# Routing tokens to experts beside a recurrence: one indirect DMA at a time, expert weights by register-addressed loads, uneven blocks

## The chip, the cores and the metric

The kernel runs on one core of a Trainium2 chip. Such a core has five engines that run their own instruction streams: TensorE (PE; its weight loads are shown as PEld), VectorE (DVE), ScalarE (ACT), GpSimd (POOL) and SyncE (SP). Semaphores order them. DMAs are issued from an engine's queue; here SP and ACT issue plain ones, POOL the indirect ones, whose row addresses come from a tile in SBUF. The metric is the device time of one execution in microseconds (us), lower is better. The granted TensorE clock is shown by the profile as a share of full speed (PEclk).

## The reference, cut to what matters

The whole program is two transformer-like layers. The change touches only its last stage, a recurrence (8 batches by 512 steps, width 256) followed by a mixture of 16 experts, of which each token uses two.

```python
def _L1_cond2_ref(x, h0, Wx, Wh, b):
    xW = jnp.einsum('ntd,dh->nth', x, Wx) + b
    def step(h_prev, xw_t):
        h_next = jnp.tanh(xw_t + h_prev @ Wh)
        return (h_next, h_next)
    _, hs = jax.lax.scan(step, h0, jnp.swapaxes(xW, 0, 1))
    return jnp.swapaxes(hs, 0, 1)

def _L1_ffn_ref(x, gate_w, gate_b, shared_wg, shared_wu, shared_wd, experts_wg, experts_wu, experts_wd):
    router_logits = jax.nn.sigmoid(x @ gate_w + gate_b)
    expert_values, expert_indices = jax.lax.top_k(router_logits, k=2)
    expert_values = expert_values / jnp.sum(expert_values, axis=-1, keepdims=True)
    hg = jnp.einsum('bsd,edi->bsei', x, experts_wg)
    hu = jnp.einsum('bsd,edi->bsei', x, experts_wu)
    all_outputs = jnp.einsum('bsei,eid->bsed', jax.nn.silu(hg) * hu, experts_wd)
    selected = jnp.take_along_axis(all_outputs, expert_indices[..., None], axis=2)
    expert_weighted = jnp.sum(expert_values[..., None] * selected, axis=2)
    return x + _mlp(x, shared_wg, shared_wu, shared_wd) + expert_weighted
```

The recurrence is strictly serial in time. The experts need only its outputs, so they can run on an earlier stretch of time while later steps are computed. Each of 8 x 512 = 4096 tokens goes to two experts: 8192 rows of 256 numbers.

## The kernel before

All earlier stages end shortly before 3779 us of the profile's span and stay as they are, except that line numbers shift. The last stage is `rnn_moe`.

**A step.** `rnn_step` issues for each time step 8 small products on PE (L1272, 16 matmul records in fp32), a tanh on ACT (L1276) and a 32-wise transposition on DVE (L1277) that writes the new state into a ring; the next step's products wait for that transposition. `rnn_seed` (L1256) loads the next step's input term into PSUM ahead of time. So one step is a loop PE, ACT, DVE, PE.

**Pieces between steps.** Everything else is written as Python generators that are advanced once after each step. A generator that yields 1 has put a piece of PE work behind this step; one that yields 0 has not. After each step one piece of `ranks`, one of `gathers`, and one of `chunks` or, when that gives no PE work, of `big` is taken. The order on PE, ACT and DVE is exactly the order in which this is written; SP and POOL take their instructions in program order too. What a piece wants done on ACT or DVE is put off with `later` to the time just after the next step.

- `rnn_project`: the input product of each later chunk of 16 steps (2 pieces each).
- `Experts.chunk`: for 16 finished steps (128 tokens): POOL copies the state into `hT` (L1308) and the input into `xc` (L1235); PE computes the router logits, turns the state to rows (`hr`, L1326) and computes the shared expert: 4 pieces, the result in `acc`.
- `Experts.rank`: for a block of `TB` = 128 steps (8 chunks, 1024 tokens): DVE counts tokens for each expert and computes `row`, the place of each token in a list sorted by expert in tiles of 128 rows, `wrow`, the row of a tile's weights, and `tw`, the mixing weights. In its middle it issues 16 scatters in one go (L1421, POOL, 128 rows of 1 KB each into the DRAM tensor `xs`).
- `Experts.tiles`: (2 x 1024 + 16 x 127) / 128 = 31 tiles a block. A tile is fetched three tiles ahead: its weights `w` (128 x 768 numbers, 384 KB) by an indirect DMA on POOL (L1456), its rows `x` (128 KB) by SP (L1460). Three pieces a tile: `gate` for k = 0 and k = 1 (L1475, 128 x 256 products), each with half the turning of the next tile's `x` (L1466), and a third with `down` of the tile two before (L1494) and `back`, which turns the activation of the tile before (L1488). SP stores the result (L1499, `ys`).
- `Experts.collect`: the two rows of each token are gathered from `ys` (L1533, POOL, two at a time), added to `acc` with the mixing weights (L1541, DVE), and stored (L1545, SP).

When the 512 steps are over, a loop without steps takes the pieces that are left. At the start of the stage ACT fills both `xs` tensors with zeros (L1562).

Of the kernel before, what the change touches and what calls it, by code (L numbers as in the profile page):

```python
# [18 lines left out]
P = 128  # L19
# [6 lines left out]
TB = 128  # L26
# [1201 lines left out]
NB = S // TB  # L1228
# [10 lines left out]
def rnn_project(K, M):  # L1239

    for n in range(1, S // XB):
        xc = chunk_x(K, M, n, "xp")
        yield 0
        px = M.psx.tile([P, D], F32, name="px", tag="px")
        for k in range(2):
            K.nc.tensor.matmul(px, xc[:, k], M.wx[:, k, :], start=(k == 0), stop=(k == 1))
            if k == 1:
                M.later(lambda n=n, px=px: K.nc.vector.tensor_tensor(M.xw[:, n, :], px, M.rbias, ALU.add))
            yield 1
# [11 lines left out]
def rnn_step(K, M, t):  # L1261
# [15 lines left out]
    nc.vector.transpose(M.ring[:, at].rearrange("p k b -> p (k b)"), h)  # L1277


class Experts:  # L1280
# [11 lines left out]
    def __init__(self, K, M, nb):  # L1292
        self.K, self.M, self.nb = K, M, nb
        self.xs, self.ys = M.xs[nb % 2], M.ys[nb % 2]
        self.hr, self.acc = [], []
        self.top, self.topi = self.rp("top", [8, 8]), self.rp("topi", [8, 8], U32)

    def rp(self, name, shape, dt=F32):
        return self.M.rp.tile([P] + shape, dt, name=name, tag=name)

    def chunk(self, c, ring):
# [3 lines left out]
        t0 = self.nb * TB + c * XB  # L1305
# [11 lines left out]
        for k in range(2):  # L1317
            nc.tensor.transpose(pt[:, k, :], hk[k], K.ident)
        hr = M.ap.tile([P, D], F32, name="hr", tag="hr", bufs=18)
        self.hr.append(hr)  # L1320
        rl = M.sp.tile([P, NE], F32, name="rl", tag="rl")

        def logits():
            nc.vector.tensor_tensor(rl, pr, M.rb, ALU.add)
            nc.scalar.activation(rl, rl, AF.Sigmoid)
            nc.scalar.copy(hr, po[:, 0:D])  # L1326

        later(logits)
        pw = M.pgu.tile([P, 2, P], F32, name="pw", tag="gu")
# [7 lines left out]
        def act():  # L1337
            nc.scalar.activation(a, pw[:, 0], AF.Sigmoid)
            nc.vector.max(out=self.top[:, c, :], in_=rl)
            nc.vector.max_index(out=self.topi[:, c, :], in_max=self.top[:, c, :], in_values=rl)  # L1340
            nc.vector.tensor_tensor(a, pw[:, 0], a, ALU.mult)
# [12 lines left out]
        acc = M.ap.tile([P, D], F32, name="acc", tag="acc", bufs=22)  # L1354
# [11 lines left out]
    def rank(self):  # L1366

        K, M, NE, NT, rp, top = self.K, self.M, self.NE, self.M.NT, self.rp, self.top
        nc, mm, C = K.nc, K.nc.tensor.matmul, TB // XB
# [16 lines left out]
        for d in (1, 2, 4):  # L1386
# [30 lines left out]

        group = f"scatter{self.nb}"
        for c in range(C):
            for i in range(2):  # L1420
                w = nc.gpsimd.indirect_dma_start(  # L1421
                    out=self.xs[:, :],
                    out_offset=bass.IndirectOffsetOnAxis(ap=self.row[:, c, i : i + 1], axis=0),
                    in_=self.hr[c],
                    in_offset=None,
                )
                K.tc.declare_no_dep(w.ins, group=group, reason="rows of their own")
                K.tc.add_to_no_dep_group(group, w.ins)
        yield 0

        le = M.rp.tile([P, NT, NE], F32, name="le", tag="le", bufs=1)
        nc.vector.tensor_tensor(le, end.unsqueeze(1).to_broadcast([P, NT, NE]), M.tile.unsqueeze(2).to_broadcast([P, NT, NE]), ALU.is_le)
# [14 lines left out]

    def tiles(self):

        K, M, NT = self.K, self.M, self.M.NT  # L1450
# [3 lines left out]
        def fetch(m):  # L1454
            W[m] = M.wp.tile([P, 768], F32, name="w", tag="w")
            nc.gpsimd.indirect_dma_start(  # L1456
                out=W[m], out_offset=None, in_=M.experts, in_offset=bass.IndirectOffsetOnAxis(ap=self.wrow[:, m : m + 1], axis=0)
            )
# [13 lines left out]
        def gate(m, k):  # L1472
            if k == 0:
                G[m] = M.pgu.tile([P, 2, P], F32, name="pg", tag="gu")
            mm(G[m].rearrange("p g i -> p (g i)"), X[m][:, k, :], W[m][:, k * D : (k + 1) * D], start=(k == 0), stop=(k == 1))  # L1475
            if k == 1:
                X.pop(m)
                later(lambda: act(m, G.pop(m)))

        def act(m, pg):  # L1480
            a = A[m] = M.sp.tile([P, P], F32, name="ea", tag="ea")
            nc.scalar.activation(a, pg[:, 0, :], AF.Sigmoid)
            nc.vector.tensor_tensor(a, pg[:, 0, :], a, ALU.mult)
            nc.vector.tensor_tensor(a, pg[:, 1, :], a, ALU.mult)

        def back(m):
            pa = M.pd.tile([P, P], F32, name="pa", tag="pd")
            nc.tensor.transpose(pa, A.pop(m), K.ident)  # L1488
            aT = A[m] = M.sp.tile([P, P], F32, name="aT", tag="aT")
            later(lambda: nc.vector.tensor_copy(aT, pa))  # L1490

        def down(m):
            py = M.pd.tile([P, D], F32, name="py", tag="pd")
            mm(py, A.pop(m), W.pop(m)[:, 2 * D : 3 * D], start=True, stop=True)  # L1494
# [10 lines left out]
        yield 1  # L1505
# [3 lines left out]
        for m in range(NT + 2):  # L1509
            for n in range(3):  # L1510
# [5 lines left out]
                if n == 2:  # L1516
                    if 0 <= m - 2 < NT:
                        down(m - 2)
                    if 0 <= m - 1 < NT:
                        back(m - 1)  # L1520
# [4 lines left out]
    def collect(self):  # L1525

        K, M, nc = self.K, self.M, self.K.nc
        C, Y = TB // XB, {}
        for c in range(C + 2):
            if c < C:  # L1530
                for i in range(2):
                    y = Y[c, i] = M.sp.tile([P, D], F32, name="yg", tag="yg", bufs=6)
                    nc.gpsimd.indirect_dma_start(  # L1533
                        out=y, out_offset=None, in_=self.ys[:, :], in_offset=bass.IndirectOffsetOnAxis(ap=self.row[:, c, i : i + 1], axis=0)
                    )
            yield 0
            yield 0
            if c > 1:
                acc = self.acc[c - 2]
                for i in range(2):  # L1540
                    nc.vector.scalar_tensor_tensor(acc, Y.pop((c - 2, i)), self.tw[:, c - 2, i : i + 1], acc, ALU.mult, ALU.add)  # L1541
                    if i == 0:
                        yield 0
                t0 = self.nb * TB + (c - 2) * XB
# [3 lines left out]
def rnn_moe(K, out):  # L1548
# [3 lines left out]
    with ExitStack() as es:  # L1552
        wp = K.pool(es, "m_w")
        M = Scope()
        M.NT = (2 * B * TB + 16 * (P - 1)) // P
# [74 lines left out]
        def ranked(x):  # L1630
            yield from x.rank()
            for _ in range(20):
                yield 0
# [5 lines left out]

        with K.tc.manual_schedule(engines={E.PE, E.Activation, E.DVE}):  # L1640
            for t in range(S):
                at = t % XB
                if t % TB == 0:
                    blk = Experts(K, M, t // TB)
                rnn_step(K, M, t)
                consume()

                advance(ranks)
                advance(gathers)
                advance(chunks) or advance(big)  # L1650
                if at == XB - 1:
                    chunks.append(blk.chunk(t % TB // XB, M.ring))
                    if t % TB == TB - 1:
                        def late(x=blk, ring=M.ring):
                            yield from x.chunk(TB // XB - 1, ring)
                            ranks.append(ranked(x))
                        chunks[-1] = late()
            while chunks or ranks or big or gathers:
# [3 lines left out]
                advance(chunks) or advance(big)  # L1662
            consume()
# [170 lines left out]
```

## Time and profile before

| what | us |
|---|---|
| median of 3 runs (4696.21 to 4704.57) | 4701.56 |
| the profiled execution | 4710.34 |
| its span, first to last instruction | 4708.6 |
| first to last transposition of the step loop, L1277 x512 | 3779.0 to 4548.7 |
| from there to the end of the span | 160 |

The last stage has these operations on POOL, by the groups of that engine from 3779 us on: 124 weight fetches L1456 (mean 963 ns, 119.4 us), 64 scatters L1421 (966 ns, 61.8 us), 64 gathers L1533 (959 ns, 61.4 us), and copies of 0.29 to 0.41 us each. In the timeline each row is start, duration, engine, line, what it writes and reads, and in brackets how long the engine was idle before it and who ended that. In a table of windows each row is a stretch of time, its length, and for each engine busy time and, in brackets, the number of instructions, then the granted clock, the DMA engines' busy share and GB/s. A DMA_INDIRECT row on POOL is the time in which POOL makes the descriptors, not the transfer.

### The profile page before, as it was taken

How to read it: one execution, taken by the hardware profiler on the slowest of the kernel's cores; microseconds unless marked ns; L12 is line 12 of the kernel's file. 1: busy time of each engine (PE TensorE's matmuls, PEld its weight loads, DVE VectorE, ACT ScalarE, POOL GpSimd, SP SyncE). 2: the span in 40 equal slices, each digit the busy share in tenths (PEclk: the TensorE clock that was granted, in tenths of full speed). 3: DMA queues.
4: the chain of work that ended last, by engine and by line, in shares of the span. 5: the costliest groups of instructions: out<-in, count | busy, mean ns of one | idle time of the engine just before them, and what ended most of it. 6: DMA issues, size and time to landing. Idle time of an engine off the chain costs nothing.

```text
span 4708.6 us, 121113 instructions
## 1 busy us (share of the span) xinstructions
PE 3497.0 (74%) x51178; PEld 2153.2 (46%) x51178; DVE 2179.5 (46%) x7763; ACT 1309.7 (28%) x4703; POOL 1019.4 (22%) x1658
## 2 busy tenths in 40 slices
PE   8700067777766767478889999999999976879675
PEld 5400044444444444345545555555555554546453
DVE  3300045555554444444547666667666632334333
ACT  2100012222222222133434334433433321323233
POOL 0177500000000000042102222222222112132434
PEclk9855589999999999989989999999999997989897
DMA  2100000000000000100000000000000021334356
GB/s 77 37 1 1 0 16 17 17 17 12 12 3 3 3 3 3 55 24 20 9 2 1 1 1 1 1 1 1 1 1 1 1 81 48 101 110 135 118 150 223
DMA packets 94415, 153.88 MB, mean 33 GB/s; under 512 B 21264, under 2 KB 72240, under 8 KB 93488
## 3 DMA queue, kind: packets, MB, share of 16 engines
q0 software_dynamic: 28352, 72.05, 5.4%
q1 hardware_dynamic: 54208, 59.69, 4.0%
q10 hardware_dynamic: 11312, 14.42, 0.9%
q8 instruction: 401, 6.57, 0.6%
q14 instruction: 142, 1.16, 0.1%
HBM read 107.82 MB, written 39.45 MB: 31 GB/s over the span
## 4 chain that ended last, share of the span: by engine, by line
PE 53%; DVE 20%; another core or an unknown queue 9%; ACT 8%; issue 7%; DMA 1%; ACTq 0%; POOL 0%; SPq 0%; DVEq 0%; POOLq 0%
PE pga L630 9%; PE pg L1272 5%; PE pe L1108 4%; DVE G L636 4%; PE po L1162 3%; PE pt L1147 3%; PE pp L1075 3%; ACT X L637 3%; PE pv L1093 3%; ACT th L646 2%; PE px L1178 2%; PE pg L1475 2%; DVE pr L642 2%; DVE ring L647 2%
## 5 line engine op out<-in xcount | busy, mean ns | idle before, releaser
L630 PE MATMUL pga<-wh,ring 128*8 128x192 f32 x8176 | 427.8, 327 | 382.2 <-DVE ring L647 367.3
L630 PEld LDWEIGHTS pga<-wh,ring 128*8 128x8 f32 x8176 | 171.9, 88 | 632.7 <-DVE ring L647 578.6
L1277 DVE STREAM_TRANSPOSE ring<-h 128x64 f32<-128x64 f32 x512 | 125.6, 245 | 518.2 <-ACT h L1276 482.3
L636 DVE STREAM_TRANSPOSE G<-pga 128x192 f32<-128x192 f32 x512 | 196.5, 384 | 364.0 <-PE pga L630 364.0
L1128 ACT ACTIVATE sm<-sm,nm 128x388 f32<-128x388 f32 (+3 forms) x512 | 283.6, 555 | 252.5 <-DVE nm L1124 251.0
L637 ACT ACTIVATE X<-G 128x48 f32<-128x48 f32 x512 | 124.1, 242 | 812.9 <-DVE G L636 805.6
L1272 PE MATMUL pg<-wh,ring 128*8 128x64 f32 x8176 | 220.6, 229 | 125.5 <-DVE ring L1277 80.7
L442 PE MATMUL pA<-ohl,ohh 128*32 128x16 f32 x512 | 29.9, 215 | 369.9 <-DVE ohl L439 283.2
L1075 PE MATMUL pp<-hn,wqkv 128*128 128x512 f32 x512 | 281.4, 690 | 10.9 <-DVE hn L1061 10.9
L1276 ACT ACTIVATE h<-pg 128x64 f32<-128x64 f32 x512 | 114.8, 224 | 590.9 <-PE pg L1272 443.1
L421 POOL DMA_INDIRECT gath<-sdr,idx x256 | 253.3, 990 | 99.3 <-issue 77.8
L1137 POOL COPY pme<-sm 128x4 f32<-128x4 f32 x512 | 127.2, 248 | 654.1 <-DVE sm L1133 650.0
L607 PE MATMUL pga<-xw,ident 128*8 128x192 f32 x4096 | 261.5, 326 | 0.5 <-DVE xw L601 0.5
L1108 PE MATMUL pe<-kt,qt 32*128 32x132 f32 (+3 forms) x2048 | 259.2, 472 | 0.1
L1147 PE MATMUL pt<-ident,sm 128*128 128x128 f32 x1280 | 211.5, 287 | 45.7 <-DVE eT L1149 45.5
L1272 PEld LDWEIGHTS pg<-wh,ring 128*8 128x8 f32 x8176 | 122.6, 91 | 252.6 <-DVE ring L1277 142.2
L1147 PEld LDWEIGHTS pt<-ident,sm 128*128 128x128 f32 x1280 | 151.4, 146 | 165.7 <-DVE eT L1149 77.2
L1162 PE MATMUL po<-eT,v 128*64 128x128 f32 x2560 | 206.1, 281 | 17.2 <-DVE rr L1079 15.3
L630 PE MATMUL pgo<-wh,ring 128*8 128x64 f32 x8176 | 207.7, 219 | 0.0
L1133 DVE TENSOR_SCALAR sm<-sm,rc 128x388 f32<-128x388 f32 (+3 forms) x512 | 200.0, 433 | 5.2
L657 POOL TENSOR_SCALAR hT<-ring 128x128 f32<-128x128 f32 x64 | 41.0, 641 | 732.6 <-DVE ring L647 732.6
L442 PEld LDWEIGHTS pA<-ohl,ohh 128*32 128x32 f32 x512 | 28.4, 156 | 372.1 <-DVE ohl L439 284.5
(490 smaller groups left out, 7287.9 us busy)
## 6 DMA issues: line engine op xcount, KB each, us to landing
x<-xs SPq DMA_DIRECT2D x124, 128.0 KB
ys<-y SPq DMA_DIRECT2D x124, 128.0 KB
w<-in_ada_w_dram SPq DMA_DIRECT2D x16, 512.0 KB
xs<-zero ACTq DMA_DIRECT2D x2, 3968.0 KB
gath<-sdr,idx POOLq DMA_INDIRECT x256
out_dram<-acc SPq DMA_DIRECT2D x32, 128.0 KB
wqkv<-in_w_qkvT_dram SPq DMA_DIRECT2D x1, 3072.0 KB
et<-in_x_dram SPq DMA_DIRECT2D x4, 512.0 KB
```

The costliest lines, as they stand in the source:

```text
L421: nc.gpsimd.indirect_dma_start(out=gath[:, c : c + 1], out_offset=None, in_=sdr[:, :], in_offset=bass.IndirectOffsetOnAxis(ap=idx[:, c : c ...
L607: mm(pga[t % 2][32 * j : 32 * j + B], pick[:, tt, :], xw[:, j * 256 : j * 256 + 192], start=True, stop=False)
L630: mm(dst[32 * j : 32 * j + B], hp, wh[:, k, j * 256 + lo : j * 256 + hi], start=False, stop=(k == 1))
L636: nc.vector.transpose(G[:, 0:3].rearrange("p g k b -> p (g k b)"), a.rearrange("p g n -> p (g n)"))
L637: nc.scalar.activation(X[:, 0:3], G[:, 0:3, :, 0:B], AF.Tanh)
L1075: mm(pp, T.wqkv[:, k, 0 : 2048].rearrange("p (i g h n) -> p i g h n", i=2, g=4, h=2)[:, i, g, h], self.hn[b][:, k, :], start=(k == 0), sto ...
L1108: mm(pe[a][:, 0 : w - lo], q[r, h, at], k[r, h, lo:w], start=(h == 0), stop=(h == 1))
L1128: nc.scalar.activation(sm[a][:, 0:w], sm[a][:, 0:w], AF.Exp, bias=nm[:, a : a + 1], scale=-1.0, accum_out=su[:, a : a + 1])
L1133: nc.vector.tensor_scalar(sm[a][:, 0:w], sm[a][:, 0:w], rc[:, a : a + 1], None, ALU.mult)
L1147: nc.tensor.transpose(pt[:, j, :], sm[a][:, 4 + j * P : 4 + (j + 1) * P], K.ident)
L1162: mm(po[64 * f : 64 * f + 64, pr, :], v[:, j, 64 * a : 64 * a + 64], eT[a][:, j, :], start=(j == 0), stop=(j == c))
L1272: mm(pg[32 * j : 32 * j + B], hp, M.wh[:, k, 64 * j : 64 * j + 64], start=False, stop=(k == 1))
```

## The change

1. Blocks are no longer of 8 chunks each but of 6, 8, 11 and 7. The tiles of a block are 27, 31, 37 and 29, again 124. The scratch tensors `xs` and `ys` are sized for the largest, 37 tiles.
2. Scatters move from the middle of `rank` to its end and are issued one at a time, with two yields after each. Each one also gets a dependency on `M.pace`, the transposition of the step just issued (in the loop without steps: the last `down` product). In the built program this is a POOL wait for that DVE instruction. The wait of 20 yields before the tiles of a block becomes 4.
3. Gathers are issued one at a time too, with the same dependency and two more yields after each while other work is left.
4. The weights of a tile are no longer fetched by an indirect DMA on POOL. SP reads the row number from `wrow` into a register and issues a plain DMA from that address. In the built program this is one TensorLoad, three register instructions and one DMA on SP for each tile, ahead of the load of `x`.
5. `gate` computes [inner, row] instead of [row, inner]: the weights are the stationary operand, four products of 128 x 128 for each tile instead of two of 128 x 256. The turning of the activation (`back`, L1488, and the DVE copy L1490) goes away, and `down` comes one tile earlier. The activation's first two operations run after the first gate piece.
6. A chunk has five pieces: the turning of the state is a piece of its own with the first product of the shared expert, and the choice of the top two moves there. Buffers of `hr` go from 18 to 16, of `acc` from 22 to 27. `rnn_project` copies its input one chunk ahead.

```diff
+BLOCKS = (6, 8, 11, 7)
-    nc.vector.transpose(M.ring[:, at].rearrange("p k b -> p (k b)"), h)
+    M.pace = nc.vector.transpose(M.ring[:, at].rearrange("p k b -> p (k b)"), h)
...
+    def paced(self, dma):
+        info = mybir.DependencyInfo(mybir.DependencyClass.Sync, mybir.DependencyReason.SCHED_ONLY)
+        self.K.tc.add_manual_dep(dma.ins, self.M.pace.ins.name, info, reason="one at a time")
...
+        group = f"scatter{self.nb}"
+        for c in range(C):
+            for i in range(2):
+                w = nc.gpsimd.indirect_dma_start(
...
+                self.paced(w)
+                K.tc.declare_no_dep(w.ins, group=group, reason="rows of their own")
+                K.tc.add_to_no_dep_group(group, w.ins)
+                yield 0
+                yield 0
...
         def fetch(m):
             W[m] = M.wp.tile([P, 768], F32, name="w", tag="w")
-            nc.gpsimd.indirect_dma_start(
-                out=W[m], out_offset=None, in_=M.experts, in_offset=bass.IndirectOffsetOnAxis(ap=self.wrow[:, m : m + 1], axis=0)
-            )
+            row = nc.sync.value_load(self.wrow[0:1, m : m + 1], min_val=0, max_val=(self.NE - 1) * P)
+            nc.sync.dma_start(out=W[m], in_=M.experts[bass.ds(row, P), :])
             X[m] = M.sp.tile([P, D], F32, name="x", tag="x")
             nc.sync.dma_start(out=X[m], in_=self.xs[m * P : (m + 1) * P, :])
...
-        def gate(m, k):
-            if k == 0:
+        def gate(m, g):
+            if g == 0:
                 G[m] = M.pgu.tile([P, 2, P], F32, name="pg", tag="gu")
-            mm(G[m].rearrange("p g i -> p (g i)"), X[m][:, k, :], W[m][:, k * D : (k + 1) * D], start=(k == 0), stop=(k == 1))
+            pg = G[m]
+            for k in range(2):
+                mm(pg[:, g], W[m][:, k * D + g * P : k * D + (g + 1) * P], X[m][:, k, :], start=(k == 0), stop=(k == 1))
...
-        def back(m):
-            pa = M.pd.tile([P, P], F32, name="pa", tag="pd")
-            nc.tensor.transpose(pa, A.pop(m), K.ident)
-            aT = A[m] = M.sp.tile([P, P], F32, name="aT", tag="aT")
-            later(lambda: nc.vector.tensor_copy(aT, pa))
...
-            mm(py, A.pop(m), W.pop(m)[:, 2 * D : 3 * D], start=True, stop=True)
+            M.last = mm(py, A.pop(m), W.pop(m)[:, 2 * D : 3 * D], start=True, stop=True)
...
         for c in range(C + 2):
-            if c < C:
-                for i in range(2):
+            for i in range(2):
+                if c < C:
                     y = Y[c, i] = M.sp.tile([P, D], F32, name="yg", tag="yg", bufs=6)
-                    nc.gpsimd.indirect_dma_start(
...
+                    self.paced(
+                        nc.gpsimd.indirect_dma_start(
...
+                    for _ in range(2 if M.left else 0):
+                        yield 0
...
-        M.NT = (2 * B * TB + 16 * (P - 1)) // P
+        M.NT = 2 * max(BLOCKS) + 15
...
             yield from x.rank()
-            for _ in range(20):
+            for _ in range(4):
                 yield 0
```

## The prediction

> **What bounds the kernel now.** Everything up to 3779 us of the span stays, so only the last 930 us count: 770 us of steps (the transpositions L1277 run from 3779.0 to 4548.7) and 160 us after them. A step is a serial loop PE, ACT, DVE, so I read the timeline first, for what delays the tanh L1276. Rows: start, duration, what, and in brackets the idle time before and its releaser.
>
> ```profile
> 4052.90 0.41 PE L1272 MATMUL pg<-wh,ring 128*8 128x64 f32 x16
> 4053.13 0.94 POOL L1456 DMA_INDIRECT w<-in_experts_dram,wrow  x1 [3.53 <-PE pa L1488]
> 4053.76 0.22 ACT L1276 ACTIVATE h<-pg 128x64 f32<-128x64 f32 x1 [1.02 <-PE pg L1272]
> ...
> 4056.69 0.41 PE L1272 MATMUL pg<-wh,ring 128*8 128x64 f32 x16
> 4056.93 0.94 POOL L1456 DMA_INDIRECT w<-in_experts_dram,wrow  x1 [2.85 <-PE pa L1488]
> 4058.26 0.22 ACT L1276 ACTIVATE h<-pg 128x64 f32<-128x64 f32 x1 [1.73 <-PE pg L1272]
> ```
>
> Without POOL the tanh follows the products' end within 0.07 us (products of 4067.42 end at 4067.83, tanh 4067.90). Here it starts 0.45 us after their end (4053.31) and 1.16 us after it (4057.10): 0.63 and 1.33 us after POOL began an indirect DMA. PE's completion gets through at one of these two moments, not while descriptors are made. When the products end 0.17 us after POOL's start, about 45 times it is the first moment, some ten times the second (each single indirect DMA between steps lined up with its tanh); when they end 0.4 us or more after it, nearly always the second. Back to back there is hardly a moment left:
>
> ```profile
> 3956.93 0.22 ACT L1276 ACTIVATE h<-pg 128x64 f32<-128x64 f32 x1 [4.93 <-remote]
> 3957.29 0.96 POOL L1421 DMA_INDIRECT xs<-hr,row  x1 [0.30 <-DMA xs<-hr,row]
> ...
> 3973.78 0.95 POOL L1456 DMA_INDIRECT w<-in_experts_dram,wrow  x1 [0.31 <-issue]
> 3978.18 0.22 ACT L1276 ACTIVATE h<-pg 128x64 f32<-128x64 f32 x1 [20.86 <-remote]
> ```
>
> The 16 scatters and four weight fetches leave two steps in 27 us. To size it I take windows restricted to L1277, so that the count in brackets is steps (then clock, DMA share, GB/s):
>
> ```profile
> 3948.00:3993.00 45.00, 3.54 (x15) 0.57 0.28 95
> ...
> 4153.00:4190.00 37.00, 2.94 (x12) 0.72 0.33 105
> ...
> 4215.00:4255.00 40.00, 4.66 (x19) 0.80 0.37 107
> 4255.00:4364.00 109.00, 20.12 (x82) 1.00 0.47 135
> 4364.00:4400.00 36.00, 2.45 (x10) 0.67 0.29 92
> ...
> 4427.00:4470.00 43.00, 5.14 (x21) 0.88 0.41 121
> ```
>
> Three stretches with scatters and two with gathers: 201 us for 77 steps. The stretch from 4255 shows the same mix of work without either: 109/82 = 1.33 us a step. The PE clock also falls to about half after each stall. The 160 us after the steps, whole engines (PE, PEld, DVE, ACT, POOL):
>
> ```profile
> 4549.00:4573.50 24.50, 21.02 (x113) 15.17 (x113) 14.70 (x65) 10.93 (x39) 13.37 (x15) 1.00 0.69 219
> 4573.50:4597.30 23.80, 4.91 (x15) 2.38 (x13) 2.04 (x7) 2.64 (x9) 13.55 (x15) 0.61 0.50 166
> 4597.30:4634.00 36.70, 20.81 (x66) 13.34 (x67) 12.57 (x36) 7.50 (x29) 22.39 (x23) 0.65 0.64 186
> 4634.00:4679.00 45.00, 42.78 (x213) 29.25 (x211) 19.02 (x73) 27.38 (x95) 18.00 (x19) 1.00 0.90 321
> 4679.00:4708.60 29.60, 0.00 (x0) 0.00 (x0) 7.75 (x16) 0.15 (x1) 15.18 (x16) 0.54 0.39 112
> ```
>
> Leftover tiles; a dead stretch (scatters of the last block); a slow one (gathers in bursts); a steady one; the last 16 gathers with no PE work. In the steady one a tile takes 1.8 us (25 stores `ys` in 45 us), PE is 95% busy and the DMAs are at their limit: 4640 to 4665 showed 360 GB/s, and a tile moves 384 + 128 + 128 KB = 655 kB, 1.8 us at that rate.
>
> **The change part by part.**
>
> *Bursts go.* 201 - 77 x 1.33 = 99 us, the clock's fall included.
>
> *Weight fetches leave POOL.* 89 run between steps, 16 of them in the stretches above. The stretch from 4255 has 20 in 82 steps. Without them I build it from shorter rows: a step 1.03, a gate step 1.19, a chunk's first two pieces 1.49 and 1.38: 16 steps 18.8 us, 82 steps 96.5. So a fetch costs 12.5/20 = 0.62 us, in line with delays of 0.45 and 1.16. 73 x 0.62 = 45 us.
>
> *What comes back.* 50 scatters and 28 gathers still fall between steps (blocks 0 to 2; gathers of blocks 0 and 1). Each now waits for a transposition, as the step's products do. POOL starts an indirect DMA about 0.23 us after its releaser (wait over at 4641.40, start 4641.62), the products end 0.47 us after the transposition: 0.2 to 0.25 after POOL's start, the case of the rows above. So mostly the first moment: (45 x 0.44 + 10 x 1.16)/55 = 0.57 us, 78 x 0.57 = +44 us. Ends: 0.3 each (+23), or always the second moment, 1.16 (+90). Queued behind a paced DMA on POOL are the copies `hT` and `xc`; they have two yields of slack, and PE waits for them if a gather blocks on a store.
>
> A rule speaks against this whole account: the Trainium skill, "SBUF — State Buffer", section "SBUF: two separate sides", says that PE never waits on anyone at SBUF and that the shared port hurts GpSimd's own descriptor writing instead. By it, spreading the scatters frees only POOL's queue, and the 99 us would shrink to what POOL copies wait; I would give 20. The rows say otherwise: tanh waits for PE's semaphore alone, and that comes 20 us late. I go by the rows.
>
> *Zero fill.* 37 instead of 31 tiles for two tensors: 9.5 instead of 7.9 MB. ACT sits 8.8 us in the second fill's issue, and the first tanh (3778.71) waits for ACT. The extra 1.6 MB at 370 GB/s (3770 to 3780) adds 4 us.
>
> *Pieces.* Chunks take 31 more slots in the loop at about the same sum of PE time (the heavy first piece is split), and longer ranks with spread scatters delay the tiles of block 2: 84 tile pieces instead of 33 are left after the steps. That is some 50 fewer pieces beside steps, two in three a gate of 0.16 us: -5 us. The gate's four 128-column products replace two of 256: 512 columns either way; `back` saves one 0.27 us product and a DVE copy of 0.25, both hidden beside steps; if that cover went, 124 x 0.27 = 33 us. `rnn_project`, `topi` and buffer counts: nothing, they lie in slots of 1.03 us steps whose PE is free half the time.
>
> *After the steps.* 57 tiles (28 of block 2, 29 of block 3) instead of 43. The dead stretch goes, since block 3 is ranked and scattered beside block 2's tiles. By DMA: 57 x 655 kB, 14 scatters, 22 gathers and 11 stores of 131 kB: 43.5 MB at 360 GB/s, 121 us. Between the blocks SP can only fetch after the last store of block 2: 4 us. The last gathers: 14 instead of 16 at 1.25 us each, 27. Sum 152. But SP now issues three DMAs a tile at 0.32 (rows of `x` and `ys`), the register load T and three register instructions (0.05 each assumed): 1.11 + T a tile. No row shows T. Below, it costs no less than a DMA issue, 0.32. The Trainium skill, "DMA: Bandwidth & Descriptors", section "Latency and other measured facts", gives a floor of about 600 ns for a tensor load: with 0.6 SP needs 1.71 a tile and DMA still rules, 152; by the nearest row 152 too. I take T = 1.0, since the DMA that uses the register must wait for it in order: 57 x 2.11 + 11 output stores of 0.61 + 34 = 161. Against 160: +1. Ends 0.32 (-8) and 1.6 (+35).
>
> *Sum against the profiled execution:* -99 - 45 + 44 + 4 - 5 + 1 = -100: 4710.3 becomes 4610. The profiled run lies 8.8 us above the median of the three, so the median becomes 4602.
>
> **The rivals.**
>
> *Each paced DMA costs the second moment* (chance 0.16). For it: gathers (L1533) with products ending 0.37 us or later after POOL's start took 1.2 us and more. Against: the releaser's 0.23 us fits the early case. 78 x (1.16 - 0.57) = +46: 4648.
>
> *SP becomes the bound after the steps, and the kernel is slower* (0.12). Every tile passes through one in-order queue: load, weights, rows, store; the store waits for ACT's copy, and the next load for the store. The gain of 100 between the steps is eaten when 57 x (1.11 + T) + 41 reaches 261, T = 2.7 us. At T = 3 it is 275, so +14: 4716. For it: no such load has been timed here, and all 57 tiles need one. Against: a floor of 0.6.
>
> *The pacing does nothing, because the delay sits in the transfers* (0.05): the stalls of the scatters return in pieces, 78 x 1.35 = 105 us instead of 44: 4663. Against: the single fetches show two fixed moments. The built program does hold the waits.
>
> **How the numbers follow.** Forecast 0.67, with its own range 4570 to 4640 (0.3 or 0.9 us a paced DMA: -21 to +26; T: -8 to +15). 8 in 10: low 4560 (0.3 each, tail -8, a better clock between steps, about -15 more), high 4680 (second moment and T = 1.6: +46 +34). Under 0.2% (9 us) no change can be told. Faster is the forecast, the first and third rival: 0.86; same 0.02; slower 0.12.
>
> **What would show it.** No tanh wait over 3 us between the steps, no "remote" rows of 20 us. Stretches with scatters at 1.5 to 1.7 us a step. POOL's L1421 and L1533 start 0.2 us after a transposition, tanh 0.6 after that. The first step 4 us later. After the steps 2.1 us a tile, SP without a gap, and no dead stretch. I am wrong if the tanh comes 1.33 us after each paced DMA, if a register load takes over 2 us, or if PE waits for `w` or `x` between steps because SP's queue is held by a store.

## The result and the profile after

| | before | after |
|---|---|---|
| median, us (20 runs each) | 4704.80 | 4714.76 |
| profiled execution (span) | 4710.34 (4708.6) | 4707.05 (4705.1) |
| step loop, first to last transposition | 769.8 (3779.0 to 4548.7) | 741.4 (3774.6 to 4516.0) |
| after the steps | 160 | 189 |
| tiles after the steps, median us from one to the next | 1.77 | 2.39 |
| delay of the tanh behind its products beyond 0.07 us, summed over the steps where it is over 0.3 | 141 | 29 |

The ratio is 1.0018, 95% interval 1.0009 to 1.0026: slower by 0.2%, where 4602 was forecast. The profiled execution of after lies 8 us below its median, that of before 6 us above, so the traces differ by -3 us and the medians by +10. The last two rows are worked out from the traces; the delay is the start of each tanh minus the end of its 16 product records.

The long stalls, which the change was to remove, are gone. The waits of ACT before the tanh in the step loop (who was waited for: us in total, times, longest; "remote" is a releaser that the profile cannot name), first of before, then of after:

```profile
ACT h L1276 <- remote: 79.2, 9, 20.9
```

```profile
ACT h L1277 <- PE pg L1273: 525.6, 500, 2.5
...
ACT h L1277 <- PE pw L1352: 3.6, 1, 3.6
```

Nine waits, 79 us together and one of them 20.9, have become nothing: the longest wait of any kind is 3.6. A paced scatter of after in the timeline (start, duration, engine, what, idle before and releaser):

```profile
3957.84 0.24 DVE L1278 STREAM_TRANSPOSE ring<-h 128x64 f32<-128x64 f32 x1 [0.99 <-ACT h L1277]
3958.14 0.61 PE L1273 MATMUL pg<-wh,ring 128*8 128x64 f32 x16 [0.41 <-DVE ring L1278]
3958.36 0.95 POOL L1455 DMA_INDIRECT xs<-hr,row  x1 [1.67 <-DVE ring L1278]
3958.96 0.22 ACT L1277 ACTIVATE h<-pg 128x64 f32<-128x64 f32 x1 [1.15 <-PE pg L1273]
```

POOL starts 0.28 us after the transposition, the tanh 0.60 after POOL: the first of the two moments, as forecast. Not all do so: of the 56 tanhs whose products end within 1 us after an indirect DMA began, 33 start by 0.66 us after it and 23 only at 1.28 to 1.69, the second moment. The windows restricted to the transposition L1278 (length, busy time and in brackets the number of steps, clock, DMA share, GB/s), three with indirect DMAs and one, from 4220, without any:

```profile
3945.00:3983.00 38.00, 6.13 (x25) 0.54 0.34 116
4124.00:4180.00 56.00, 8.34 (x34) 0.79 0.39 118
4220.00:4370.00 150.00, 27.25 (x112) 1.00 0.33 99
4376.00:4458.00 82.00, 11.28 (x46) 0.56 0.33 106
```

With indirect DMAs a step takes 1.52, 1.65 and 1.78 us, where before had two steps in 27 us. The clock, though, is at about half in two of these stretches without a long stall; below full it is for 194 us of the loop, for 151 before. And the quiet stretch takes 150/112 = 1.34 us a step. Before took 1.33 there with a weight fetch in every fourth step, and without fetches 96.5/82 = 1.18 was forecast. Something costs about 0.16 us a step where POOL does nothing. The timeline of that mix of work shows it:

```profile
4051.40 0.24 DVE L1278 STREAM_TRANSPOSE ring<-h 128x64 f32<-128x64 f32 x1 [0.89 <-ACT h L1277]
...
4051.57 0.29 DVE L1502 TENSOR_TENSOR ea<-pg,ea 128x128 f32<-128x128 f32 x1
...
4051.92 0.71 PE L1496 MATMUL pg<-xT,w 128*128 128x128 f32 x4 [0.72 <-DVE ea L1502]
...
4052.67 0.41 PE L1273 MATMUL pg<-wh,ring 128*8 128x64 f32 x16
...
4053.14 0.22 ACT L1277 ACTIVATE h<-pg 128x64 f32<-128x64 f32 x1 [1.45 <-PE pg L1273]
```

The transposition ends at 4051.64, and the next step's products could start then. They start at 4052.67: the second half of the gate stands ahead of them on PE, and it has itself waited 0.72 us for a DVE operation that comes after the transposition. This step takes 2.0 us. The waits of PE in the step loop of after say how often:

```profile
PE pg L1496 <- DVE ea L1502: 41.1, 53, 1.7
PE px L1247 <- DVE xw L1249: 22.1, 24, 1.1
PE po L1337 <- DVE rl L1331: 18.6, 31, 1.2
```

82 us in 108 waits, of three kinds with one pattern. A piece writes a PSUM tile; the read is put off with `later` to after the next step's transposition; and the next piece writes **another part of the same tile**, or the next tile in the same single buffer. The first half of the gate and its `silu`, then the second half. The router's logits, then the turning, both in `po`. The last product of one `px`, then the first product of the next, since the change took out the yield 0 that lay between them. The second write then waits for the read of the first part, as the releasers in these lines say. Before, both halves of a gate were written ahead of one read, the turning stood in the same piece as the logits, and a yield of 0 parted two `px`.

After the steps, whole engines (PE, PEld, DVE, ACT, POOL, then clock, DMA share, GB/s):

```profile
4516.00:4560.00 44.00, 33.01 (x214) 27.87 (x213) 16.69 (x70) 17.74 (x66) 14.19 (x16) 0.96 0.85 256
4560.00:4600.00 40.00, 29.97 (x197) 24.60 (x197) 9.34 (x32) 17.05 (x64) 3.83 (x4) 1.00 0.87 260
4600.00:4640.00 40.00, 28.45 (x155) 23.12 (x154) 12.29 (x38) 14.85 (x51) 12.28 (x13) 0.87 0.86 262
4640.00:4675.00 35.00, 22.95 (x135) 18.37 (x134) 10.43 (x32) 13.04 (x45) 4.73 (x5) 0.95 0.82 249
4675.00:4705.10 30.10, 3.13 (x18) 2.12 (x17) 7.65 (x17) 1.66 (x5) 13.24 (x14) 0.62 0.37 107
```

The dead stretch is gone and the work is even. But where before's steady stretch moved 321 GB/s at a DMA share of 0.90, here it is 249 to 262 at 0.82 to 0.87. PE is not full either (33 of 44 us). From the first result to the last it takes 161 us, where 121 by DMA and 4 between the blocks were forecast. Two waits stand side by side, that of PE for DVE between the two halves of a gate (4516 to 4640), and those of SP's queue (4516 to 4675):

```profile
PE pg L1496 <- DVE ea L1502: 16.4, 27, 1.4
```

```profile
SPq L1478 <- PE pt L1484: 21.8, 21, 3.0
SPq L1518 <- ACT ea L1501: 7.3, 7, 2.8
SPq L1518 <- ACT xT L1485: 7.2, 19, 0.6
...
SPq L1518 <- ACT y L1517: 6.4, 6, 1.9
```

The first is the wait of the step loop again. From 4561 to 4587 eleven tiles take 2.39 us each, and in each PE stands still for 0.58 us before the second half of the gate, while SP waits for PE to free a buffer of `x`. So there the gate's wait sets the pace. The other one is the store (L1518), 21 us in all, which waits for ACT while the next tile's weights and rows stand behind it.

### The profile page after: what moved, and what is told of

Read it like the earlier page. It is cut to its first block, busy times and chain, and to the rows that moved or that the text cites. A ratio compares the mean times of both kernels' runs of the same rounds, so it can differ in the third digit from the quotient of the medians.

```text
span 4705.1 us, 122302 instructions
## 1 busy us (share of the span) xinstructions
PE 3502.3 (74%) x51550; PEld 2195.2 (47%) x51550; DVE 2148.3 (46%) x7641; ACT 1313.6 (28%) x4703; POOL 897.2 (19%) x1534
## 4 chain that ended last, share of the span: by engine, by line
PE 53%; DVE 21%; ACT 9%; another core or an unknown queue 7%; issue 7%; DMA 1%; ACTq 1%; POOL 0%; SPq 0%; DVEq 0%; POOLq 0%
PE pga L629 9%; PE pg L1273 5%; DVE G L635 4%; PE pe L1107 4%; PE po L1161 3%; PE pg L1496 3%; PE pt L1146 3%; PE pp L1074 3%; ACT X L636 3%; PE pv L1092 3%; ACT th L645 2%; PE px L1177 2%; DVE pr L641 2%; DVE ring L646 2%
## 5 line engine op out<-in xcount | busy, mean ns | idle before, releaser
L1278 DVE STREAM_TRANSPOSE ring<-h 128x64 f32<-128x64 f32 x512 | 125.6, 245 | 524.3 <-ACT h L1277 509.6
L1273 PE MATMUL pg<-wh,ring 128*8 128x64 f32 x8176 | 231.5, 238 | 71.5 <-DVE ring L1278 63.1
L1496 PE MATMUL pg<-xT,w 128*128 128x128 f32 x992 | 176.7, 302 | 67.1 <-DVE ea L1502 59.1
```

What stands on the lines that cost most here:

```text
L1273: mm(pg[32 * j : 32 * j + B], hp, M.wh[:, k, 64 * j : 64 * j + 64], start=False, stop=(k == 1))
L1496: mm(pg[:, g], W[m][:, k * D + g * P : k * D + (g + 1) * P], X[m][:, k, :], start=(k == 0), stop=(k == 1))
```

## The experiments

The two suspects are tried apart: the waits for PSUM reads between the steps, and SP's queue after them. In the numbers below, "loop" is first to last transposition and "after the steps" from there to the end of the last addition into `acc`, some 4 us before the end of the span (so before has 155.3 on this scale and the changed kernel 185.5), both of the profiled run; ratios are to the kernel before, timed on the same chip. A ratio of 0.001 is 4.7 us.

**The three waits, one at a time and together.** `e1_project` puts both `px` products into one piece and a slot without PE work after it:

```diff
             if k == 1:
                 M.later(lambda n=n, px=px: ...)
-            yield 1
+        yield 1
+        yield 0
```

> The changed kernel with the two products of the input projection in one piece and an empty slot after it, so that PE never asks for the single-buffered px in the step in which DVE still has to read it. Theory W (PE waits for DVE's late read of the PSUM tile that it writes next): about 30 steps of 2.03 us in the first 100 become 1.1 and 1.2, minus 20 to 30 us. Rival P (the paced indirect DMAs eat the gain): no indirect DMA lies in these steps, so whatever the time does here says nothing for P; if W is wrong the time stays within 5 us.

Measured: ratio 0.9972 (0.9963 to 0.9981), 22 us under the changed kernel's 1.0018; loop 727. `e2_silu` reads the gate once, when both halves are written:

```diff
-            if g == 0:
+            if g == 1:
+                X.pop(m)
+                G.pop(m)
                 a = A[m] = M.sp.tile([P, P], F32, name="ea", tag="ea")
                 def silu():
                     nc.scalar.activation(a, pg[:, 0], AF.Sigmoid)
                     nc.vector.tensor_tensor(a, pg[:, 0], a, ALU.mult)
+                    nc.vector.tensor_tensor(a, pg[:, 1], a, ALU.mult)
                 later(silu)
-            else:
...
```

> The changed kernel with the activation's sigmoid and first product put off until both gate pieces are written, as before the change. Theory W: the second gate piece no longer waits for DVE's read of the first half; 70 tiles beside steps gain 0.8 us each (minus 55) and the tiles after the steps go from 2.4 to 1.8 us (57 of them, minus 35): minus 90 in all. Rival S (SP's queue of loads, weights, rows and stores sets the tile after the steps): only minus 55, and the tile stays at 2.4 us. Rival P: no change beyond 20 us.

Measured: 0.9917 (0.9898 to 0.9936), 48 us less; loop 695. After the steps nothing changed (185 us, 2.50 a tile), as Rival S had it, although the gate's wait is gone there too: in its place the store waits 36 us for ACT (21 before the edit), and PE 30.5 us for rows of `x` (18.8). `e3_chunk4` moves the turning back into the router's piece, four pieces a chunk:

```diff
         for k in range(2):
             mm(pr, hk[k], M.wr[:, k, :], start=(k == 0), stop=(k == 1))
...
-        later(logits)
-        yield 1
         for k in range(2):
             nc.tensor.transpose(pt[:, k, :], hk[k], K.ident)
+        later(logits)
```

> The changed kernel with the turning of the state back in the piece of the router logits, so four pieces a chunk. Theory W: the turning no longer waits for DVE's read of the logits in the same PSUM tile; 32 steps of 1.74 become about 1.5 and the slot goes to a tile: minus 10 to 20 us. If the split was worth what it looks like (a lighter first piece), plus 5 instead.

Measured: 0.9999 (0.9990 to 1.0008), 9 us less, only just clear of the noise; loop 731. `e4_all` has all three edits.

> The three edits together. Theory W: the sum, minus 120 to 140, near 4580. Rival P: at most minus 40. Rival S: minus 90, with the tile after the steps at 2.4 us.

Measured: 0.9867 (0.9849 to 0.9885), 71 us less; loop 679, after the steps 182 with 2.56 us a tile. Single effects of 22, 48 and 9 us make 79 together, so they hardly overlap. The 120 to 140 expected did not come: 35 of them were to lie after the steps. The windows restricted to the transposition show for `e4_all`, in a stretch without indirect DMAs:

```profile
4182.00:4312.00 130.00, 26.97 (x110) 1.00 0.41 122
```

130/110 = 1.18 us a step: the forecast for this mix of work, to the second digit. In the waits of PE between the steps none of the three kinds is left. The part of the theory that lay between the steps is shown. After the steps taking these waits out gave 3 us (185.5 to 182), so something else holds the tiles as soon as they are gone.

**What holds the tiles after the steps.** The next four kernels are `e4_all` with one thing changed. `e5_pool_w` gives the weight fetch back to POOL:

```diff
-            row = nc.sync.value_load(self.wrow[0:1, m : m + 1], ...)
-            nc.sync.dma_start(out=W[m], in_=M.experts[bass.ds(row, P), :])
+            nc.gpsimd.indirect_dma_start(out=W[m], ..., in_offset=...(ap=self.wrow[:, m : m + 1], axis=0))
```

> Base: the kernel with all three edits (ratio 0.9867, 4651 us; loop 679, after the steps 182 with 2.56 us a tile); one part of the change is undone: the weights of a tile are again fetched by an indirect DMA on POOL, all else as there. Theory W (the move of the weights to SP's queue costs after the steps what it gains between them): about 73 fetches between steps at 0.62 us, loop 679 + 45 = 724; the tile after the steps falls from 2.56 to 1.8 to 1.9 us, so some 54 x 0.65 = 35 us less there: 182 becomes 147; sum +10, ratio 0.989. Rival P (after the steps the new order of PE's products or the two blocks' tiles set the 2.5 us, not the fetch): loop 724, tile stays 2.4 or more: +45, ratio 0.996. Rival N (a fetch on POOL costs nothing beside steps): loop 680.

Measured: 0.9961 (0.9949 to 0.9974); loop 715, so +36 where 45 were expected; after the steps 187 with 2.32 us a tile. Theory W was right about the loop and wrong about the tail; the total is what Rival P said. Its timeline, restricted to POOL, has a reason:

```profile
4590.25 0.95 POOL L1475 DMA_INDIRECT w<-in_experts_dram,wrow  x1 [0.30 <-issue]
4591.50 0.95 POOL L1549 DMA_INDIRECT yg<-ys,row  x1 [0.30 <-issue]
4592.75 0.95 POOL L1475 DMA_INDIRECT w<-in_experts_dram,wrow  x1 [0.30 <-issue]
4594.00 0.95 POOL L1549 DMA_INDIRECT yg<-ys,row  x1 [0.30 <-issue]
```

Fetches and gathers are back to back on POOL, a burst again, beside which ACT and PE wait for "remote" and "issue". The two cases can be told apart: where no scatter or gather falls between two results after the steps, the median from one to the next is 1.75 us here, against 2.45 in `e4_all` and 1.77 before; where one does it is 2.99, against 2.70 in `e4_all`. So the move to SP's queue did cost the quiet tiles what Theory W said, and the other ones take the gain back. In the total the fetch on SP is worth its place. `e6_ahead` fetches five tiles ahead with six buffers of `x`:

```diff
-            X[m] = M.sp.tile([P, D], F32, name="x", tag="x")
+            X[m] = M.sp.tile([P, D], F32, name="x", tag="x", bufs=6)
...
-                    if m + 3 < NT:
-                        fetch(m + 3)
+                    if m + 5 < NT:
+                        fetch(m + 5)
```

> Base as in the run before: all three edits, weights by SP. Only the distance of the fetch changes: five tiles ahead instead of three, six buffers of x instead of four. Theory D (too few bytes in flight: weights and rows lie behind the store of a tile in SP's order, and three tiles are 1.5 MB): the tile after the steps falls from 2.56 to 2.0 us or less, 182 becomes some 155, ratio 0.981. Theory E (the DMA engines themselves move less: 3072-byte packets of one queue at a mean of 164 ns, 18.7 bytes a ns, where POOL's had 22.9): tile stays 2.4 to 2.5, after the steps 178 to 184, ratio 0.986.

Measured: 0.9852 (0.9836 to 0.9869); 2.21 us a tile, 171 after the steps: between the two theories. `e7_ys_act` lets ACT issue the store that holds SP:

```diff
-                nc.sync.dma_start(out=self.ys[m * P : (m + 1) * P, :], in_=y)
+                nc.scalar.dma_start(out=self.ys[m * P : (m + 1) * P, :], in_=y)
```

> Base as before: all three edits, weights by SP, three tiles ahead. Only the store of a tile's result (ys) is issued by ACT, which made it, instead of SP. Theory D (SP's queue is held by the store, 29 us of waits for ACT's copy): SP runs ahead until the four buffers of x stop it, tile 2.0 to 2.2 us, after the steps some 160, ratio 0.982 or a little more because ACT issues 124 DMAs of 0.3 us. Theory E with one queue as the cause (the packets of one queue run one after the other, those of two overlap): stores overlap with the weights, tile about 2.2. Theory E with the packets as the cause: tile 2.4 to 2.5, ratio 0.986 to 0.988.

Measured: 0.9850 (0.9833 to 0.9866); loop 679 as in `e4_all`, after the steps 165 with 1.94 us a tile, about what Theory D said. In the medians less of it shows: its profiled execution lies 14 us below the three others, and the ratio is 8 us under that of `e4_all`, with intervals that overlap. The largest wait of a tile's DMAs in SP's queue after the steps, first of `e4_all`, then of `e7_ys_act`, and third a wait of PE in `e4_all`:

```profile
SPq L1516 <- ACT y L1515: 28.9, 28, 3.7
```

```profile
SPq L1478 <- PE pt L1484: 22.1, 20, 2.3
```

```profile
PE pt L1484 <- DMA x<-xs: 35.2, 30, 3.4
```

In `e4_all` the store waits 28.9 us for ACT's copy, and the next tile's weights and rows stand behind it; PE waits for these rows (the third line), in `e7_ys_act` 15.6 us instead of 35.2. In `e7_ys_act` the load of `x` waits until PE has freed a buffer: SP now runs ahead as far as buffers go. And the DMAs fill up; one of its windows (as above):

```profile
4500.00:4540.00 40.00, 33.27 (x216) 28.50 (x215) 11.00 (x38) 20.20 (x72) 6.67 (x7) 0.96 0.97 324
```

324 GB/s at a share of 0.97, against 321 at 0.90 before. So Theory E may hold for a small part: 6% fewer bytes (324/0.97 = 334 against 321/0.90 = 357 GB/s) in the same busy time. In the packet records a row of weights fetched by SP is 3072 bytes, 164 ns mean and 121 median (`e4_all`), where POOL's packets of 6144 took 268 mean (before, 4634 to 4679). E is bounded, not taken away, by these runs.

**The bursts.** `e8_burst` is `e4_all` with each block's scatters in one go, not paced, after the same number of yields:

```diff
+        for _ in range(4 * C):
+            yield 0
         for c in range(C):
             for i in range(2):
                 w = nc.gpsimd.indirect_dma_start(...)
-                self.paced(w)
...
-                yield 0
-                yield 0
```

> Base as before: all three edits. Only the pacing of the scatters is undone: each block's scatters are issued in one go, without a wait for a step, after the same number of yields, so the tiles start at the same piece as before. Theory of the prediction (back to back indirect DMAs hold PE's completion for all but a few moments): the 50 scatters of blocks 0 to 2 take some 69 us of standing still instead of 50 x 0.57 = 28 us, so the loop is some 40 us longer, 679 becomes 720, ratio 0.995, with tanh waits of 10 us and more. Rival (each indirect DMA costs the same wherever it stands): loop 679, ratio 0.987. After the steps the 14 scatters of the last block go in one burst beside tiles, within 5 us of the base.

Measured: 0.9954 (0.9937 to 0.9971); loop 708, so +29 where 40 were expected; after the steps 189, +7. Its timeline, restricted to POOL and the tanh, has the picture of before:

```profile
3932.83 0.22 ACT L1278 ACTIVATE h<-pg 128x64 f32<-128x64 f32 x1 [2.55 <-PE pg L1274]
3933.53 0.96 POOL L1457 DMA_INDIRECT xs<-hr,row  x1 [0.30 <-issue]
3934.79 0.96 POOL L1457 DMA_INDIRECT xs<-hr,row  x1 [0.30 <-issue]
...
3938.60 0.96 POOL L1457 DMA_INDIRECT xs<-hr,row  x1 [0.30 <-issue]
3939.52 0.23 ACT L1278 ACTIVATE h<-pg 128x64 f32<-128x64 f32 x1 [5.62 <-remote]
```

The wait of 5.6 us, "remote", is back in its place. The waits of ACT between the steps have eleven of that kind:

```profile
ACT h L1278 <- remote: 59.4, 11, 8.3
```

The longest is 8.3 us, not 10 and more as expected. Pacing the scatters gains what it was to gain, at three quarters of the size. The pacing of the gathers was not undone alone.

**Put together.** `e9_both` has `e6_ahead` and `e7_ys_act`; `e10_equal` is `e9_both` with `BLOCKS = (8, 8, 8, 8)`; `e11_one` is `e10_equal` with one `yield 0` after a scatter instead of two.

> Base: the three edits and the stores ys issued by ACT (ratio 0.985; loop 679, after the steps 165 at 1.94 us a tile). Added: the fetch five tiles ahead with six buffers of x. If waiting for bytes in flight is all that is left above the 1.82 us that 655 kB take at 360 GB/s, the tile falls to 1.80 to 1.85, after the steps some 159, ratio 0.984. If the packets of SP's queue are what is slower, 1.94 stays, ratio 0.985 to 0.986.

> The run before with equal blocks (8, 8, 8, 8) instead of (6, 8, 11, 7): the uneven blocks are undone. By counting pieces 46 tiles are left after the steps instead of 57, with 32 gathers instead of 36 and 16 scatters instead of 14. Theory (the uneven blocks leave more tiles behind, each at its full price there and at almost none beside a step): 11 x 1.9 = 21 us less after the steps, some 4 more between them, two more gathers at the end (+2.5): ratio 0.984 becomes 0.981. Rival (the uneven blocks avoid a dead stretch between the last two blocks): the dead stretch comes back with 15 to 20 us, ratio 0.984.

> The run before with one yield after each scatter instead of two, so that one is issued in every step and a block's tiles start 16 steps earlier; 42 tiles are left. Theory (each paced DMA costs about 0.5 us by itself, whatever its neighbours do): 4 x 1.9 = 7.5 us less after the steps, ratio 0.0015 lower. Rival (two in neighbouring steps delay each other, as the burst does): 48 x 0.5 more between the steps, ratio 0.004 higher.

These three ran on a chip on which the kernel before took 4502 us instead of 4705 (last section), so their ratios stand apart: 0.9969 (0.9957 to 0.9981), 0.9912 (0.9895 to 0.9930) and 0.9951 (0.9938 to 0.9964). Among themselves: equal blocks save 25 us, of which 19 after the steps (154.9 to 135.7). One yield instead of two loses 18 us, 11 of them in the loop (645 against 634), although fewer tiles are left after the steps. That is the direction of that run's rival but not its mechanism: on this chip the tanh delays sum to 2.8 us against 1.9, so what the 11 us are stays open.

Four more kernels, together on one chip, put them on the scale of the others: before once more, the changed kernel once more, `e10_equal` as `e14_equal`, `e9_both` as `e15_both`.

> The kernel before, for a trace of it beside the other three. In the last three runs the kernel before took 4502 us instead of 4700 to 4716, and the tanh delays behind indirect DMAs summed to 1 to 3 us instead of 33 to 37. If those runs show a chip on which POOL's indirect DMAs do not hold PE's completions, and this call meets it again: loop of steps 640 to 670 us instead of 770, no tanh wait over 5 us, 4500 us. If it meets one like the first: loop 770, 141 us of tanh delays, 4705 us.

> The changed kernel unaltered. Where indirect DMAs hold PE's completions: ratio 1.002, loop 741, 30 to 37 us of tanh delays, after the steps 186. Where they do not, the change has nothing to gain between the steps and keeps its two costs, 62 us of waits for PSUM reads and 26 us after the steps: loop some 700 against 655, sum +65, ratio 1.012 to 1.016. Rival (the other clock of that chip makes the difference): ratio 1.002 there too.

> The kernel of e10_equal again (three edits, ys issued by ACT, fetch five ahead, equal blocks). Where indirect DMAs hold PE's completions: loop some 683, after the steps some 140, ratio 0.977 to 0.981. Where they do not: 0.991 as before.

> The kernel of e9_both again (as e14 but with the uneven blocks). Where indirect DMAs hold PE's completions: loop 680, after the steps some 157, ratio 0.982 to 0.984, so some 17 us over e14. Where they do not: 0.997.

| | median us | ratio (95%) | loop | after the steps | us a tile |
|---|---|---|---|---|---|
| e12, before | 4708.67 (one run) | | 770.0 | 153.9 | 1.77 |
| e13, the changed kernel | 4712.57 | 1.0013 (1.0005 to 1.0021) | 744.4 | 185.3 | 2.39 |
| e15, three edits, ys by ACT, five ahead | 4636.47 | 0.9848 (0.9829 to 0.9867) | 684.1 | 160.5 | 2.03 |
| e14, that with equal blocks | 4597.61 | 0.9763 (0.9747 to 0.9779) | 672.3 | 138.0 | 1.90 |

`e14_equal` beats both kernels, by 108 us against before and 115 against the changed one. Fetching farther ahead adds nothing that can be told once the store is off SP's queue (0.9848 against 0.9850). The uneven blocks cost 39 us in the medians and 34 in the profiled runs: 22.5 after the steps, where 11 tiles fewer are left (46 for 57), and 12 in the loop, where 4 more were expected, so that part is not explained. In `e14_equal` the granted clock is below full for 104 us of the loop, in `e15_both` for 210; whether that is the cause was not tried.

## Why the prediction was wrong, point by point

Both main terms had the right mechanism; the forecast failed on a step that was costed at nothing and on one that was mis-sized.

- **The step that failed: "Pieces".** It said of `rnn_project`, `topi` and buffer counts "nothing, they lie in slots of 1.03 us steps whose PE is free half the time", and of the gate's products "512 columns either way". The columns were counted, the order of writes and reads was not. PE is free half the time, but its instructions stand in order, and a piece that waits for a put-off read of its own PSUM tile holds the next step's products. Removing the three waits took 62 us out of the loop (741 to 679).
- **The mis-sized term: "After the steps", +1.** Measured +29 (160 to 189). The register load that the term turned on was the wrong worry: T was taken as 1.0 us, and the trace has 124 loads on SP with a median of 0.27 and a mean of 0.38, the shortest 0.15, where the Trainium skill gives a floor of 600 ns ("DMA: Bandwidth & Descriptors", "Latency and other measured facts"). Nor is there one beside each tile: 95 stand in three bunches between the steps, one for each of the first three blocks, and 29 after the steps, 17 us in all. SP's own rows after the steps sum to about 1.5 us a tile, less than the tile takes. What the term left out are two waits. The gate's wait sets the tile's 2.39 us where it stands in every tile; and weights that POOL used to fetch ahead now stand in SP's queue behind a store that waits for ACT. By the traces either one keeps the tile at about 2.4 us, so taking out the first alone gave 3 us; taking the store off the queue then gave 17 in the profiled runs. The store alone was not tried. The closing sentence of the prediction names the second case, "SP's queue is held by a store", but only between the steps and at no price. In the sum of that term, 34 us stand where its parts give 4 and 27.
- **Bursts and fetches, -99 and -45.** Right in kind. Undoing the pacing of the scatters in `e4_all` cost 29 in the loop where 40 were expected, undoing the move of the fetch 36 of 45. Without the waits the loop was to be 770 - 99 - 45 + 44 - 5 = 665; `e4_all` has 679, so 14 us are missing here. (Of the 89 fetches between the steps two stand at the edge of two windows and are counted twice.) One part of the 99 did not come, "the clock's fall included": the prediction put that fall down to the stalls, but in the loop of `e4_all` the clock is below full for 177 us, before for 151. Steps take 1.71 us there and 1.22 at full clock; how much of the 0.49 is the clock and how much the indirect DMAs in the same stretches was not tried.
- **Paced DMAs, +44.** The size is near, the picture half right. The tanh delays of after sum to 29 us, of `e4_all`, where no other wait hides them, to 37. In after the mean delay beside an indirect DMA is 0.57 us, 0.50 more than without, where 0.57 more was taken. But the prediction had the products end 0.2 to 0.25 us after POOL's start and nearly one in five tanhs at the second moment. They end 0.39 us after it (median), so the first moment costs only 0.29; and 23 of 56 come at the second, at 0.97. That these two errors cancel is luck.
- **Zero fill, +4.** In the first profile the steps began 4.4 us earlier than before, not later. In ten further profiles with the same fill on chips of this kind, that of `e13_after` among them, they began at 3779.7 to 3786.1, against 3778.5 and 3779.0 before. So +4 is about right as a rule, and the start scatters by as much. (The fills are 9.7 and 8.1 MB, not 9.5 and 7.9; the difference of 1.6 is right.)

The forecast for the profiled run was -100. Set right by +62 for the waits, +28 after the steps and -8 for the start, it is -18; measured were -3, and the remainder is the 14 us above, so that the sum comes out proves nothing more. The medians differ by 13 us more than the profiled runs.

Of the rivals, "SP becomes the bound" came nearest with 4716, but not by its mechanism: it needed 275 us after the steps and a load of 3 us, and there were 189 and 0.27. Its time is a coincidence of 62 us that it didn't know of. That each paced DMA costs the second moment holds for 23 of 56 and is wrong as a rule. That the delay sits in the transfers, so that pacing does nothing, is against `e8_burst`. The rule of the Trainium skill that PE never waits on anyone at SBUF was set aside for the rows, with 20 us in place of 99; undoing the pacing of the scatters alone cost 29 in the loop, so the rows were the better guide on these chips.

## What to carry to other kernels

When reads are put off behind a serial loop, list for every PSUM tile which piece writes it and in which slot it is read: a piece that writes into a tile whose read is still put off stops an in-order engine, and everything queued behind it, however idle that engine is by its busy time. When a transfer moves to another queue, price not its issue but what it now stands behind, and which engine that waits for. Where two limits stand at the same height, taking one away shows nothing until the other goes too. And a change whose main gain is real can still be worth nothing: after finding the gain in the trace, look at a stretch that the change should not have touched.

## What was not expected of the hardware

**The hold of PE's completion by an indirect DMA was there on three chips and all but missing on a fourth.** The same kernel and the same scatters, in `e14_equal` and in `e10_equal`, in the timeline:

```profile
4145.06 0.41 PE L1274 MATMUL pg<-wh,ring 128*8 128x64 f32 x16
4145.29 0.98 POOL L1455 DMA_INDIRECT xs<-hr,row  x1 [8.46 <-DVE ring L1279]
4145.87 0.23 ACT L1278 ACTIVATE h<-pg 128x64 f32<-128x64 f32 x1 [1.01 <-PE pg L1274]
```

```profile
4041.03 0.41 PE L1274 MATMUL pg<-wh,ring 128*8 128x64 f32 x16
4041.25 0.98 POOL L1455 DMA_INDIRECT xs<-hr,row  x1 [8.46 <-DVE ring L1279]
4041.55 0.22 ACT L1278 ACTIVATE h<-pg 128x64 f32<-128x64 f32 x1 [0.73 <-PE pg L1274]
```

In both, the products end 0.18 to 0.19 us after POOL's start. On the first chip the tanh comes 0.40 us after their end, on the second 0.11. Over all such products in the loop of each kernel the mean is 0.63 against 0.10 us, while POOL's rows have the same lengths. On the second chip the kernel before took 4502 us, and `e10_equal` was at its first step 96 us earlier than `e14_equal`. The two traces of the same program say where. 68 of the 96 us come between 225 and 690 us, where POOL issues 256 gathers back to back, and 25 between 1970 and 2500, where it fetches weights by indirect DMAs; in the 2460 us of the two long stretches without one, 690 to 1970 and 2500 to 3680, the lead grows by only 3. In the middle of the gathers an operation on DVE (L438) that `e10_equal` makes at 330 us comes at 577 in `e14_equal`, after the last gather. So the lead comes where indirect DMAs are, as in the recurrence.

With delays that small, pacing and the move of the fetch have little to gain there, and `e9_both` is 0.3% faster than before instead of 1.5%. How the changed kernel itself does there was not measured. One visit does not tell whether the chip or its state at that time makes the difference, and what differs stays open.
